# Gathers of a message-passing kernel that also wait for VectorE, another order of its last steps, and a smaller general path

## The chip, the cores and the metric

The kernel runs on one core of a Trainium2 chip. Its engines are TensorE (PE in the profile, with weight loads as PEld), VectorE (DVE), ScalarE (ACT), GpSimd (POOL) and SyncE (SP, which here issues DMAs). The metric is the device time of one execution in microseconds (us); lower is better. Before the change three runs took 722.56, 722.97 and 724.59 us, so the median is 722.97.

## The reference

One graph layer with a residual and a layer norm; 12,500 nodes of 128 features, 400,000 edges sorted by their destination:

```python
rbf = exp(-(distances[:, None] - centers) ** 2 / (2.0 * width * width))      # 50 centres
cut = 0.5 * (cos(pi * distances / CUTOFF) + 1.0) * (distances <= CUTOFF)
W = (silu(rbf @ fw1 + fb1) @ fw2 + fb2) * cut[:, None]
messages = (h[src] @ pw + pb) * W
agg = segment_sum(messages, dst, num_segments=num_atoms)
return h + (silu(agg @ mw1 + mb1) @ mw2 + mb2)
...
x = layernorm(x + that)
```

71,145 of the 400,000 edges lie within the cutoff of 10 in these inputs; all others contribute nothing.

## The kernel before

**Packing.** DVE reads the edge lists in seven chunks, keeps the edges within the cutoff and writes them, packed, to DRAM by seven indirect scatters of POOL. They come back as index columns (`srci`), as cosine factors (`cut`) and as places in a window of nodes (`dl`, `base_i`). Beside it PE multiplies all of x by `pw` and stores the result as `proj` in DRAM.

**Quads.** The packed edges are worked through in 139 quads (NL) of 512 edges, numbered q = 0 to 138. `fetch(q)` gathers the rows of x (the first 12 quads) or of `proj` by four indirect DMAs of 128 rows each, issued by POOL (L1069); for a dozen quads the first of the four is fetched row by row by SP or ACT instead. So POOL has 544 gathers in all, and 7 scatters. 13 buffers (`quad_sb`) take turns, and a gather waits until its buffer has been read. For each quad there are:
- `basis` and `first` (per pair of quads): ACT makes the 50 radial functions, PE the first layer (L1133); `silu` is ACT's (L1139, result `s`).
- `second(q)`: PE's second layer into one PSUM bank, a bias matmul (L1148) and four matmuls (L1151).
- `message(q)`: DVE multiplies that bank by the gathered rows (L1166; L1163 for rows fetched singly).
- `place(q)`: DVE writes four one-hot matrices of 128 edges by a window of nodes, already times `cut` (L1178).
- `sum_up(q)`: PE multiplies message by one-hot into `sums` (L1198).
- `add(q)`: DVE adds `sums` to `aggT`, the table of all nodes in SBUF, at positions loaded into registers from `base_i`. `bases_of` loads many values at once (L1207).

**Nodes.** Where all edges of a block of node tiles are summed, `node_first` (PE L1242/L1243, then ACT's silu into `zs`, L1245), `node_second` (PE L341/L344), `node_stats` (DVE L1280, L1284), `deviations` (L1291 to L1300), `scales` (L1310/L1311), `normal`, which normalizes (ACT, L1331), and `store` (L187) follow. The last blocks are those that start at node tiles 80, 84, 88, 90, 92, 94 and 96.

**Order.** The engines run their instructions in the order in which the program writes them. A planner with estimated times writes quads 0 to 131. The last seven, 132 to 138, are written out by hand, as a list of calls (L1610 to L1718): step q sums quad q, computes `second(q+2)` and places quad q+1, with node work in between. Each step begins with `house(q)`, which fetches and loads ahead.

**Banks.** `second`, `node_first` and `node_second` take their PSUM bank from a list of four free ones (`bank_167` to `bank_170`), in the order in which the program takes and frees them. The bank of `node_first` goes back to the list when its `zs` is written down, and whoever takes it next waits on the chip until ACT has read it:

```python
nc.scalar.activation(in_turn(s[:, :n], n), by_tile(pz[:, :n], n), AF.Silu)
free.append(pz)
```

**General path.** Behind the hand-written steps stands `with tc.If(some > 0, label="over")` (L1792): code for inputs with more or differently spread near edges than the packed lists hold. With these inputs it isn't entered; each engine compares and jumps over it. It is unrolled.

Of the kernel before, what the change touches and what calls it, by code (L numbers as in the profile page):

```python
# [9 lines left out]

F32 = mybir.dt.float32
BF16 = mybir.dt.bfloat16
# [3 lines left out]
OP = mybir.AluOpType  # L16
# [71 lines left out]
def kernel(  # L88
# [90 lines left out]

        return v.rearrange("f (t p) -> f t p", p=P) if n % P == 0 else v  # L180

    def node_dma(t0, sb, dr, store, n=None, eng=nc.sync):

        for a, m, k in alike(rows(t0, n)):
            d = dr[(t0 + a) * P:(t0 + a) * P + m * k].rearrange("(p t) f -> p t f", p=k)
            s = sb[:k, a:a + m]
            eng.dma_start(d, s) if store else eng.dma_start(s, d)  # L187

# [239 lines left out]
    def place_of(q):  # L428
        n, later = LATER
        return q % len(quad_sb) if q < n else later[(q - n) % len(later)]  # L430

    def before_it(q):

        return max((m for m in range(q) if place_of(m) == place_of(q)), default=-1)

    def room(q):

# [625 lines left out]
    def fetch(q, idx=None, table=None, js=range(QT)):  # L1063
        got = quad_sb[place_of(q) if q >= 0 else 0]
        for j in js:
            if q in SINGLY and j == 0:
                continue
            i = srci[:, 2 * q + j // 2, j % 2:j % 2 + 1] if idx is None else idx[:, j:j + 1]
            nc.gpsimd.indirect_dma_start(  # L1069
                out=got[:, j, :], out_offset=None, in_=proj if table is None else table,  # L1070
                in_offset=bass.IndirectOffsetOnAxis(ap=i, axis=0))
        got_of[q] = got

    def quads(o):
# [3 lines left out]
    def radial(o, lengths):  # L1078

        n = math.prod(lengths.shape) // QE  # L1080
        v = lengths.rearrange("(o h) e -> o h e", o=1)
        if o < 0:
            d = quad_sb[1].rearrange("p j f -> p (j f)")
            nc.sync.dma_start(d, v.to_broadcast([64, 2, QE]))
# [149 lines left out]

    zs_of, py_of, done = {}, {}, [0]

    def node_first(t0):

        n = sum(rows(t0))
        assert done[0] == NL or t0 * P + n <= done_to(2 * done[0])  # L1240
        pz = bank()
        nc.tensor.matmul(pz[:, :n], bias_b["mb1"][:, 0, :], ones_b[:, :n], start=True, stop=False)  # L1242
        nc.tensor.matmul(pz[:, :n], mw1_sb, aggT[:, t0 * P:t0 * P + n], start=False, stop=True)  # L1243
        s = work.tile([P, QE], F32, name="zs", tag="hp", bufs=3)
        nc.scalar.activation(in_turn(s[:, :n], n), by_tile(pz[:, :n], n), AF.Silu)  # L1245
        free.append(pz)
        zs_of[t0] = s
# [55 lines left out]
    def deviations(group, st):  # L1303
        return roots(*variances(group, st))
# [33 lines left out]
        nc.vector.memset(st, 0.0)  # L1338
        return st

    def finish(every):

        for t0 in every:
            load_x(t0)
            st = statistics()
            node_first(t0)
            node_second(t0)
            node_stats(t0, st)
            scales(*deviations([t0], st))
            normalize(*ready.pop(0))  # L1350
        store()


    begin, at_q = {}, NODES
# [279 lines left out]
    node_first(88)  # L1634
# [46 lines left out]
    sum_up(p, msg)  # L1681
    node_second(92)
    sum_up(q, message(q, (0, 1)), (0,))
    add(p)
# [32 lines left out]
    normalize(*ready.pop(0), on=(0, 1), eng=nc.scalar)  # L1717
    store()  # L1718

    def more(q):  # L1720
# [12 lines left out]
        base_of(q)  # L1733
        add(q)

    def everything():
        nc.vector.memset(aggT, 0.0)
        def again(e0, seen):

            def column(ap, dt, name):  # L1740
                t = work.tile([P, QT], dt, name=name, bufs=1)
                nc.sync.dma_start(t, ap[ds(e0, QE)].rearrange("(j p) -> p j", p=P))
                return t

            idx = column(src, I32, "idx")
            loc_i = column(dst, I32, "loc_i")
            lengths = column(edge_weight, F32, "lengths")
            loc = work.tile([P, QT], F32, name="loc", bufs=1)
            nc.vector.tensor_copy(loc, loc_i)
            wgt = work.tile([P, QT], F32, name="wgt", bufs=1)  # L1750
            near = work.tile([P, QT], F32, name="near", bufs=1)
            nc.vector.tensor_scalar(near, lengths, CUTOFF, 0.5, op0=OP.is_le, op1=OP.mult)
            if seen:
                nc.vector.memset(near[:, :seen], 0.0)
            fold(wgt, lengths, work.tile([P, QT], F32, name="fold_f", bufs=1),
                 work.tile([P, QT], I32, name="fold_i", bufs=1))
            cosine(wgt)
            nc.vector.scalar_tensor_tensor(wgt, wgt, 1.0, near, op0=OP.add, op1=OP.mult)
            fetch(-2, idx)
            radial(-1, edge_weight[ds(e0, QE)].rearrange("(o e) -> o e", o=1))  # L1760
            basis(-1)
            first(-1)
            silu(-1)
            second(-2)
            u = own(0, "msg", 0)
            for j in range(QT):
                nc.vector.tensor_scalar(u[:, j, :], pu_of[-2][:, j * H:(j + 1) * H],
                                        wgt[:, j:j + 1], None, op0=OP.mult)
            free.append(pu_of.pop(-2))
            msg = own(1, "msg", 0)  # L1770
            nc.vector.tensor_mul(msg, u, got_of.pop(-2))
            for n0 in range(0, N, WS):
                n = min(WS, N - n0)
                at = work.tile([P, QT], F32, name="at")
                nc.vector.tensor_scalar(at, loc, float(-n0), None, op0=OP.add)
                pa = bank()
                for j in range(QT):
                    hot = quad_sb[2 + j % 2].rearrange("p j f -> p (j f)")[:, :WS]
                    nc.vector.tensor_scalar(hot[:, :n], iota_n[:, :n], at[:, j:j + 1],
                                            None, op0=OP.is_equal)  # L1780
                    nc.tensor.matmul(pa[:, :n], msg[:, j, :], hot[:, :n],
                                     start=(j == 0), stop=(j == QT - 1))
                nc.vector.tensor_add(aggT[:, n0:n0 + n], aggT[:, n0:n0 + n], pa[:, :n])
# [8 lines left out]
    with tc.If(some > 0, label="over"):  # L1792
        total = nc.values_load(bad_i[0:1, 0:1], min_val=0, max_val=2 * E)
        extra = nc.values_load(bad_i[0:1, 1:2], min_val=0, max_val=E)
        with tc.If(extra > 0):
            for q in range(NL, NQ):
                more(q)
            finish(blocks)
        with tc.If(total > 0):
            everything()  # L1800


# [24 lines left out]
```

## Time and profile before

| | before |
|---|---|
| median of three runs | 722.97 us (722.56 to 724.59) |
| the profiled execution | 722.04 us, of which 720.2 us are the span of the trace |
| busy, share of the span | PE 82%, PEld 65%, DVE 78%, ACT 56%, POOL 73% |
| POOL instructions | 565 |
| TensorE clock granted, mean | 0.91 |
| moved by DMA | 91.44 MB |

The page of the profile shows one execution. It gives the busy time of each engine, then groups of instructions by line with their count, their busy time, the mean time of one in ns, and the idle time of the engine just ahead of them with what ended it; "issue" means that nothing in the profile released the instruction. The windows view gives an engine's busy time and count in stretches of the span, followed by the mean TensorE clock, the share of time for which the DMA engines were busy and GB/s. The timeline lists single instructions or short runs of alike ones: start, duration, engine, line, operation, out<-in, count, and in brackets the idle time ahead with its releaser. The view of one line gives the least, median and greatest duration in ns and the first and last start. An engine's name with a q (SPq, DVEq) is its sequencer: branches, waits, register loads, DMA issues.

### The profile page before, as it was taken

The numbers are of one execution on the slowest core, as the hardware profiler recorded it, in microseconds if no ns is written. First come the engines' busy times: TensorE is split into PE (matmuls) and PEld (weight loads), VectorE is DVE, ScalarE is ACT, GpSimd is POOL, SyncE is SP. The second block draws the span as 40 slices with busy tenths as digits, with TensorE's granted clock in tenths as the row PEclk, the third lists the DMA queues.
The fourth block names the chain that finished last, engine by engine and source line by source line (L and its number), as shares of the span: only waits on it lengthen the run. The fifth ranks groups of instructions, "written<-read, shape, count | busy, mean of one in ns | idle before, by whom it ended". The sixth has DMA issues, their size and how long they took to land.

```text
span 720.2 us, 14506 instructions
## 1 busy us (share of the span) xinstructions
PE 589.1 (82%) x3526; PEld 466.7 (65%) x3526; DVE 560.7 (78%) x1741; ACT 401.9 (56%) x569; POOL 528.8 (73%) x565
## 2 busy tenths in 40 slices
PE   6787668778988798798878997799998877978783
PEld 5676457666766576576666775577785665756663
DVE  8789999759998889989979994866855545655764
ACT  7356825144744667654644566466765742674554
POOL 6767777777777777777777777777777777777770
PEclk9799996799999899989997999699999897999997
DMA  8898453243434223443334344444443434344242
GB/s 284 264 287 264 114 159 103 59 139 83 115 103 129 86 84 86 129 131 84 86 111 118 101 114 121 131 127 126 143 121 92 142 100 113 99 142 126 56 130 77
DMA packets 54008, 91.44 MB, mean 127 GB/s; under 512 B 14273, under 2 KB 21537, under 8 KB 53915
## 3 DMA queue, kind: packets, MB, share of 16 engines
q0 software_dynamic: 17712, 36.51, 20.4%
q1 hardware_dynamic: 24916, 35.61, 15.0%
q10 hardware_dynamic: 11286, 18.31, 8.1%
q8 instruction: 29, 0.48, 0.3%
q14 instruction: 65, 0.52, 0.2%
HBM read 74.59 MB, written 15.79 MB: 125 GB/s over the span
## 4 chain that ended last, share of the span: by engine, by line
DVE 23%; PE 17%; POOL 17%; DMA 14%; issue 13%; ACT 3%; DVEq 2%; ACTq 1%; SPq 0%; POOLq 0%
POOL quad L1069 13%; DMA quad<-proj,srci 10%; DVE hot L1178 5%; PE ph L1133 4%; PE bank L1151 4%; POOL x L1069 4%; DVE msg L1166 3%; PE sums L1198 3%; PE bank L344 2%; DMA x<-proj,srci 2%; DVE aggT L1232 1%; DVEq L1207 1%; DMA pair<-packed 1%; DMA packed<-line,at_i 1%; DVE bank L516 1%
## 5 line engine op out<-in xcount | busy, mean ns | idle before, releaser
L1069 POOL DMA_INDIRECT quad<-proj,srci x402 | 382.3, 951 | 122.7 <-issue 98.3
L1151 PEld LDWEIGHTS bank<-fw_sb,s 128*128 128x128 f32 x1112 | 157.8, 205 | 56.7 <-issue 46.4
L1151 PE MATMUL bank<-fw_sb,s 128*128 128x128 f32 x1112 | 157.8, 288 | 0.0
L1133 PE MATMUL ph<-rbf,w_sb 102*128 102x512 f32 x278 | 143.8, 642 | 11.0 <-ACT s L1139 6.6
L1198 PEld LDWEIGHTS sums<-hot,msg 128*128 128x128 f32 x816 | 111.2, 203 | 48.8 <-issue 26.3
L1139 ACT ACTIVATE s<-ph 128x1024 f32<-128x1024 f32 x70 | 71.3, 1018 | 125.8 <-PE ph L1133 125.5
L1178 DVE TENSOR_SCALAR hot<-iota_n,dl,cut 128x80 f32<-128x80 f32 (+4 forms) x408 | 109.2, 341 | 23.3 <-PE sums L1198 20.0
L1198 PE MATMUL sums<-hot,msg 128*128 128x80 f32 (+4 forms) x816 | 113.4, 285 | 10.7 <-DVE msg L1166 10.4
L1069 POOL DMA_INDIRECT x<-proj,srci x94 | 90.0, 958 | 28.9 <-issue 25.9
L1148 PE MATMUL bank<-fb_b,ones_b 96*128 96x512 bf16 x139 | 56.0, 403 | 39.3 <-DVE msg L1166 22.9
L1133 PEld LDWEIGHTS ph<-rbf,w_sb 102*128 102x128 f32 x278 | 51.4, 206 | 51.0 <-issue 37.8
L1166 DVE TENSOR_TENSOR msg<-bank,quad 128x512 f32<-128x512 f32 (+1 forms) x78 | 52.4, 672 | 39.9 <-DMA quad<-proj,srci 33.6
L1232 DVE TENSOR_TENSOR aggT<-aggT,sums 128x80 f32 (+4 forms) x209 | 53.8, 258 | 29.5 <-PE sums L1198 10.4
L1117 ACT ACTIVATE rbf<-d_sb,rbf_bias,rbf_scale 102x512 f32<-102x512 f32 x70 | 56.2, 803 | 7.8 <-issue 7.8
L1069 POOL DMA_INDIRECT quad<-in_x_dram,srci x48 | 46.7, 973 | 18.0 <-issue 12.8
L344 PEld LDWEIGHTS bank<-pw_sb,xT 128*128 128x128 f32 (+1 forms) x292 | 44.1, 218 | 15.2 <-ACT xT L976 8.3
L1198 PE MATMUL sums<-quad,quad 128*128 128x128 f32 (+3 forms) x296 | 43.2, 291 | 10.8 <-DVE quad L1166 10.8
L1139 ACT ACT_TABLE_LOAD x34 | 43.6, 1283 | 15.1 <-issue 14.8
L1121 ACT ACT_TABLE_LOAD x35 | 44.9, 1283 | 11.3 <-issue 9.5
L1121 ACT ACTIVATE rbf<-rbf 102x512 f32<-102x512 f32 x70 | 44.1, 630 | 7.9 <-issue 5.5
L1198 PEld LDWEIGHTS sums<-quad,quad 128*128 128x128 f32 x296 | 39.8, 207 | 12.5 <-DVE quad L1166 12.2
L344 PE MATMUL bank<-pw_sb,xT 128*128 128x128 f32 (+1 forms) x292 | 45.0, 303 | 0.6 <-ACT xT L976 0.4
(281 smaller groups left out, 797.7 us busy)
## 6 DMA issues: line engine op xcount, KB each, us to landing
d_sb<-near_d ACTq DMA_DIRECT2D x67, 256.0 KB
row_sb<-proj SPq DMA_DIRECT2D x1024, 0.5 KB
x<-in_x_dram SPq DMA_DIRECT2D x46, 256.0 KB
row_sb<-proj ACTq DMA_DIRECT2D x512, 0.5 KB
quad<-proj,srci POOLq DMA_INDIRECT x402
proj<-hp SPq DMA_DIRECT2D x24, 256.0 KB
out_dram<-x SPq DMA_DIRECT2D x22, 256.0 KB
x<-proj,srci POOLq DMA_INDIRECT x94
```

The lines of the kernel that those rows point to most:

```text
L344: nc.tensor.matmul(to[:m, k, :], lT[:, k * P:k * P + m], w, start=False, stop=(k == a + c - 1))
L1069: nc.gpsimd.indirect_dma_start(out=got[:, j, :], out_offset=None, in_=proj if table is None else table, in_offset=bass.IndirectOffsetOnAxi ...
L1117: a = nc.scalar.activation(rbf[:u], d[:u], AF.Square, bias=rbf_bias[:u], scale=rbf_scale[:u])
L1121: nc.scalar.activation(rbf[:u], rbf[:u], AF.Exp, scale=-1.0 / (2.0 * width * width))
L1133: nc.tensor.matmul(ph[:, h, :], w1_sb[:2 * KR, h, :], rbf[:2 * KR], start=True, stop=True)
L1139: nc.scalar.activation(s[:, :n], ph[:, :n], AF.Silu)
L1148: nc.tensor.matmul(pu, ones_b[:, :P], bias_b["fb2"].rearrange("k j f -> k (j f)"), start=True, stop=False)
L1151: nc.tensor.matmul(pu[:, j * H:(j + 1) * H], s[:, j * P:(j + 1) * P], fw2_sb, start=False, stop=(j == QT - 1))
L1166: nc.vector.tensor_mul(msg[:, a:b, :], pu_of[q].rearrange("p (j f) -> p j f", j=QT)[:, a:b, :], got_of[q][:, a:b, :])
L1178: nc.vector.tensor_scalar(hot[:, j, :wide(q)], iota_n[:, :wide(q)], dl[:, at[0], at[1]], cut[:, at[0], at[1]], op0=OP.is_equal, op1=OP.mult)
L1198: nc.tensor.matmul(pa[:, k * W:k * W + wide(q)], msg[:, j, :], hot[:, j, :wide(q)], start=(j % n == 0), stop=(j % n == n - 1))
L1232: nc.vector.tensor_add(to, to, pa[:, k * W:k * W + wide(q)])
```

## The change

It has three parts.

**1. Waits.** A callback logs every DVE instruction of six kinds as the program writes it. Each gather with q from 0 to 138 gets a dependency on the DVE instruction that stands `behind(q)` places before the last one logged. The table `BACK` sets the number of places: 66 from quad 0 on, 38 from 16, 46 from 26, 38 from 39, 26 from 52, 19 from 63, 46 from 88, 14 from 102 and 8 from 111.

```diff
+BACK = ((0, 66), (16, 38), (26, 46), (39, 38), (52, 26), (63, 19), (88, 46), (102, 14),
+        (111, 8))
+UPTO = NL
+VECTORS = ("TensorScalarPtr", "TensorTensor", "CopyPredicated", "TensorReduce", "TensorCopy",
+           "BNStats")
...
+        if i.engine == mybir.EngineType.DVE and str(i.opcode) in VECTORS:
+            vectors.append(i.name)
...
-            nc.gpsimd.indirect_dma_start(
+            g = nc.gpsimd.indirect_dma_start(
...
+            if 0 <= q < UPTO and len(vectors) > behind(q):
+                tc.add_manual_dep(
+                    g.ins, vectors[-1 - behind(q)],
+                    mybir.DependencyInfo(mybir.DependencyClass.Sync, mybir.DependencyReason.DATA))
```

No engine's instruction order changes by this, up to quad 131 nothing but the waits differs. A gather that already waited for a later DVE instruction keeps its wait. Of 551 gathers and scatters 150 have other waits than before; their number in all goes from 741 to 752.

**2. The last steps.** Calls of the hand-written list stand in another order; `bases_of` loads the 14 positions of all seven quads in step 132 instead of six there and eight in step 135.

```diff
     q = NL - 7
...
-    node_second(84)
     second(q + 2)
-    bases_of([q, q + 1, q + 2])
+    bases_of(list(range(q, NL)))
     place(q + 1)
     scales(*deep.pop(0))
     add(q)
-    normal(1)
     first(octs(q))
     silu(octs(q))
+    node_second(84)
+    normal(1)
...
     sum_up(q, message(q))
-    normal(1)
     second(q + 2)
     first(octs(q))
     silu(octs(q))
+    normal(1)
     place(q + 1)
...
     sum_up(q, message(q))
+    second(q + 2)
     node_second(88)
-    second(q + 2)
     place(q + 1)
...
     sum_up(q, message(q))
+    second(q + 2)
     node_second(90)
-    second(q + 2)
-    bases_of([q, q + 1, q + 2, q + 3])
     place(q + 1)
...
     add(q)
+    node_first(92)
     scales(*dev)
-    node_first(92)
     normal(1)
-
-    tc.mark_branch_hint_location("over")
+    place(q + 2)
+
     p, q = NL - 2, NL - 1
     house(p)
-    msg = message(p)
-    place(q)
-    sum_up(p, msg)
+    sum_up(p, message(p))
```

ACT in steps 132 to 134, before (`x41` and `x42` are the normalizations of `normal`, `s` the results of `silu`, `zs_10850` that of `node_first(88)`):

```order
L1245 ACTIVATE zs_10755<-bank1_168 128x512
L1331 ACTIVATE x41_87<-x41_87,by_10795,rs_10794 128x128 x4
L1139 ACTIVATE s_10808<-ph_10805 128x1024
L1331 ACTIVATE x42_88<-x42_88,by_10795,rs_10794 128x128 x4
L1139 ACTIVATE s_10840<-ph_10838 128x512
L1245 ACTIVATE zs_10850<-bank3_170 128x256
```

and now:

```order
L1270 ACTIVATE zs_10755<-bank1_168 128x512
L1162 ACTIVATE s_10814<-ph_10811 128x1024
L1356 ACTIVATE x41_87<-x41_87,by_10806,rs_10805 128x128 x4
L1162 ACTIVATE s_10851<-ph_10849 128x512
L1356 ACTIVATE x42_88<-x42_88,by_10806,rs_10805 128x128 x4
L1270 ACTIVATE zs_10866<-bank3_170 128x256
```

Each set of four normalizations has moved behind the silu that it preceded, so that the second set stands directly ahead of the last zs.

PE from the end of step 133 through step 134, before (`mb2`, `mw2`: `node_second(88)`; `fb2`, `fw2`: `second(136)`):

```order
L1242 MATMUL bank3_170<-ones_b_130,mb1_b_134 128x256
L1243 MATMUL bank3_170<-aggT_99,mw1_sb_119 128x256
L1198 MATMUL sums_10865<-quad6_79,quad4_77 128x128 x4
L341 MATMUL bank3_170<-mb2_b_135,ones_b_130 128x256
L344 MATMUL bank3_170<-mw2_sb_120,zs_10850 128x128 x2
L1148 MATMUL bank1_168<-fb2_b_133,ones_b_130 128x512
L1151 MATMUL bank1_168<-fw2_sb_118,s_10808 128x128 x4
```

and now:

```order
L1267 MATMUL bank3_170<-ones_b_130,mb1_b_134 128x256
L1268 MATMUL bank3_170<-aggT_99,mw1_sb_119 128x256
L1221 MATMUL sums_10881<-quad6_79,quad4_77 128x128 x4
L1171 MATMUL bank3_170<-fb2_b_133,ones_b_130 128x512
L1174 MATMUL bank3_170<-fw2_sb_118,s_10814 128x128 x4
L347 MATMUL bank0_167<-mb2_b_135,ones_b_130 128x256
L350 MATMUL bank0_167<-mw2_sb_120,zs_10866 128x128 x2
```

The two have changed places, and with them the banks: `second(136)` now writes `bank3_170`, which `node_first(88)` wrote and its zs reads.

DVE in steps 136 and 137, before (`msg1_680` is the message of quad 137, `quad6_79` the one-hot of quad 138):

```order
L1310 RECIPROCAL rs_10995<-dev_10968 128x12
L1311 SCALAR_TENSOR_TENSOR by_10996<-both_m_10961,rs_10995 128x12
L1166 TENSOR_TENSOR msg1_680<-bank3_170,quad2_75 128x512
L1178 TENSOR_SCALAR quad6_79<-iota_n_145,dl_158,cut_157 128x128 x4
L1166 TENSOR_TENSOR quad4_77<-bank2_169,quad3_76 128x128
```

and now:

```order
L1335 RECIPROCAL rs_10998<-dev_10967 128x12
L1336 SCALAR_TENSOR_TENSOR by_10999<-both_m_10960,rs_10998 128x12
L1201 TENSOR_SCALAR quad6_79<-iota_n_145,dl_158,cut_157 128x128 x4
L1189 TENSOR_TENSOR msg1_680<-bank1_168,quad2_75 128x512
L1189 TENSOR_TENSOR quad4_77<-bank2_169,quad3_76 128x128
```

The one-hot of the last quad stands ahead of the message of the one before it.

**3. The general path.** `finish` (the node phases once more), the sums over windows and the walk over all edges become hardware loops, with DMAs by POOL; the label "over" and its hint are gone.

```diff
+    def finish_all():
+
+        with tc.For_i(0, N // (4 * P), 1) as block:
+            finish(0, block * (4 * P))
...
-            for n0 in range(0, N, WS):
...
+            with tc.For_i(0, N // WS, 1) as w:
...
-        with tc.For_i(0, E // QE, 1) as g:
-            again(g * QE, 0)
-        if E % QE:
-            again(E - QE, QT - E % QE // P)
-        finish(blocks)
-
-    with tc.If(some > 0, label="over"):
+        with tc.For_i(0, steps, 1) as g:
+            again(smin(g * QE, E - QE))
+
+    with tc.If(some > 0):
```

In the built program the instructions between each engine's branch and the place where it lands change from 262 to 111 on SP, from 541 to 123 on ACT, from 1083 to 174 on DVE, from 749 to 146 on PE and from 74 to 152 on POOL. POOL has four register moves more at its start. The hint left no instruction on the path that is taken.

More of the change, by code (lines that the diff above doesn't have):

```diff
@@ L9 @@
 from concourse._compat import with_exitstack
+from concourse.expressions import smin
 F32 = mybir.dt.float32
@@ L434, in before_it, with logged, behind @@
         return max((m for m in range(q) if place_of(m) == place_of(q)), default=-1)
+    vectors = []
+    def logged(i):
+        if i.engine == mybir.EngineType.DVE and str(i.opcode) in VECTORS:
+            vectors.append(i.name)
+    nc.push_inst_callback(logged)
+    def behind(q):
+        return next(n for at, n in reversed(BACK) if q >= at)
     def room(q):
@@ L1083, in radial @@
             d = quad_sb[1].rearrange("p j f -> p (j f)")
-            nc.sync.dma_start(d, v.to_broadcast([64, 2, QE]))
+            nc.gpsimd.dma_start(d, v.to_broadcast([64, 2, QE]))
         else:
@@ L1235, with node_first @@
     zs_of, py_of, done = {}, {}, [0]
-    def node_first(t0):
+    def node_first(t0, sums=None):
         n = sum(rows(t0))
-        assert done[0] == NL or t0 * P + n <= done_to(2 * done[0])
+        if sums is None:
+            assert done[0] == NL or t0 * P + n <= done_to(2 * done[0])
+            sums = aggT[:, t0 * P:t0 * P + n]
         pz = bank()
         nc.tensor.matmul(pz[:, :n], bias_b["mb1"][:, 0, :], ones_b[:, :n], start=True, stop=False)
-        nc.tensor.matmul(pz[:, :n], mw1_sb, aggT[:, t0 * P:t0 * P + n], start=False, stop=True)
+        nc.tensor.matmul(pz[:, :n], mw1_sb, sums, start=False, stop=True)
         s = work.tile([P, QE], F32, name="zs", tag="hp", bufs=3)
@@ L1339, in statistics, with finish @@
         return st
[L1341 to L1351, printed above, removed]
+    def finish(t0, at):
+        n = sum(rows(t0))
+        y = x_sb[t0] = x4_sb[0]
+        node_dma(t0, y, x, False, eng=nc.gpsimd, at=at)
+        sums = quad_sb[OTHERS[0]].rearrange("p j f -> p (j f)")[:, :n]
+        nc.vector.tensor_copy(sums, aggT[:, ds(at, n)])
+        st = statistics()
+        node_first(t0, sums)
+        node_second(t0)
+        node_stats(t0, st)
+        scales(*deviations([t0], st))
+        _, rs, by = ready.pop(0)
+        for k in range(len(rows(t0))):
+            scaled(t0, y, rs, by, k, False)
+        node_dma(t0, x_sb.pop(t0), out, True, eng=nc.gpsimd, at=at)
+    def finish_all():
+        with tc.For_i(0, N // (4 * P), 1) as block:
+            finish(0, block * (4 * P))
+        if N % (4 * P):
+            t0 = N // (4 * P) * 4
+            finish(t0, t0 * P)
     begin, at_q = {}, NODES
@@ L1718 @@
     store()
+    nc.remove_inst_callback(logged)
     def more(q):
@@ L1737, in everything, with again @@
         nc.vector.memset(aggT, 0.0)
-        def again(e0, seen):
+        steps, seen = -(-E // QE), -E % QE // P
+        left = work.tile([P, 1], F32, name="left", bufs=1)
+        nc.vector.memset(left, float(steps - 1))
+        def again(e0):
             def column(ap, dt, name):
                 t = work.tile([P, QT], dt, name=name, bufs=1)
-                nc.sync.dma_start(t, ap[ds(e0, QE)].rearrange("(j p) -> p j", p=P))
+                nc.gpsimd.dma_start(t, ap[ds(e0, QE)].rearrange("(j p) -> p j", p=P))
                 return t
@@ L1753, in again @@
             if seen:
-                nc.vector.memset(near[:, :seen], 0.0)
+                last = work.tile([P, 1], F32, name="last", bufs=1)
+                nc.vector.tensor_scalar(last, left, 1.0, None, op0=OP.min)
+                nc.vector.tensor_scalar(near[:, :seen], near[:, :seen], last, None, op0=OP.mult)
+                nc.vector.tensor_scalar(left, left, -1.0, None, op0=OP.add)
             fold(wgt, lengths, work.tile([P, QT], F32, name="fold_f", bufs=1),
@@ L1771, in again @@
             nc.vector.tensor_mul(msg, u, got_of.pop(-2))
-            for n0 in range(0, N, WS):
-                n = min(WS, N - n0)
-                at = work.tile([P, QT], F32, name="at")
-                nc.vector.tensor_scalar(at, loc, float(-n0), None, op0=OP.add)
+            assert N % WS == 0
+            with tc.For_i(0, N // WS, 1) as w:
                 pa = bank()
@@ L1778, in again @@
                     hot = quad_sb[2 + j % 2].rearrange("p j f -> p (j f)")[:, :WS]
[L1779 to L1783, printed above, removed]
-                free.append(pa)
-        with tc.For_i(0, E // QE, 1) as g:
-            again(g * QE, 0)
-        if E % QE:
-            again(E - QE, QT - E % QE // P)
-        finish(blocks)
-    with tc.If(some > 0, label="over"):
+                    nc.vector.tensor_scalar(hot, iota_n, loc[:, j:j + 1], None, op0=OP.is_equal)
+                    nc.tensor.matmul(pa[:, :WS], msg[:, j, :], hot, start=(j == 0),
+                                     stop=(j == QT - 1))
+                to = aggT[:, ds(w * WS, WS)]
+                nc.vector.tensor_add(to, to, pa[:, :WS])
+                nc.vector.tensor_scalar(loc, loc, -float(WS), None, op0=OP.add)
+                free.append(pa)
+        with tc.For_i(0, steps, 1) as g:
+            again(smin(g * QE, E - QE))
+    with tc.If(some > 0):
         total = nc.values_load(bad_i[0:1, 0:1], min_val=0, max_val=2 * E)
```

6 lines of the change are left out of this document (3 added, 3 removed).

## The prediction

> **What bounds the kernel now.** I read the page's costliest groups first, then the windows view for the gather line alone.
>
> ```profile
> L1069 POOL DMA_INDIRECT quad<-proj,srci x402 | 382.3, 951 | 122.7 <-issue 98.3
> 100.00:200.00 100.00, 74.58 (x80) 0.85 0.35 96
> ...
> 600.00:700.00 100.00, 75.61 (x81) 0.91 0.39 108
> L1069 POOL DMA_INDIRECT quad<-proj,srci x402: 940/945/1254, 73.1 to 702.3; - x134
> ```
>
> In the first row the idle time ahead of a gather is put down to "issue": nothing released it, it is POOL's own gap. A gather takes 0.945 us (the median of the last row), and a window of 100 us holds 80 or 81 of them at its two ends, so one comes every 1.25 us with 0.30 us of gap. POOL therefore sets the pace from the first gathers to 702.3 us, whatever DVE, PE and ACT do in between, and TensorE's clock (0.85 and 0.91 in the same rows) matters little there. Only what follows the last gathers, some 20 us, is bound by other things.
>
> The program's own time here is 722.04 us for a span of 720.2 us. The median of the runs shown is 722.97, 0.93 us above the profiled execution. I sum on 722.04 and add 0.93 at the end.
>
> **Part 1: the waits on VectorE.** POOL issues the same gathers in the same order. The built programs differ in the waits of 150 gathers: each of these now waits for a later DVE instruction than its buffer asks for. What is behind a gather on POOL is nothing but more gathers, so a wait that ends late shifts all that follow. I laid each newly named DVE instruction beside its gather; the narrowest place is this one:
>
> ```profile
> 672.87 0.68 DVE L1280 SCALAR_TENSOR_TENSOR x<-x,bank 128x512 f32<-128x512 f32 x1
> 679.67 0.95 POOL L1069 DMA_INDIRECT quad<-proj,srci  x1 [0.30 <-DVE by L1311]
> ```
>
> The DVE instruction ends at 673.55, 6.1 us before the gather starts. Elsewhere the margin is larger. The gather above keeps the usual gap of 0.30 us, as gathers without a DVE event ahead of them do, so a wait that is already met costs nothing. Term: **0**. Its bounds: 0 while DVE stays within 6.1 us of its place beside POOL, and beyond that one microsecond for each further one (rival C). A gain is excluded: the gap of 0.30 us stays, and a wait makes no gather shorter.
>
> **Part 2: the order of the last steps.** A step bears the number of its quad, 132 to 138. In steps 132 and 133:
>
> ```profile
> 680.77 0.60 ACT L1245 ACTIVATE zs<-bank 128x512 f32<-128x512 f32 x1
> 681.42 0.38 PE L341 MATMUL bank<-mb_b,ones_b 96*128 96x512 bf16 x1 [2.28 <-ACT zs L1245]
> 682.39 1.10 DVE L1178 TENSOR_SCALAR quad<-iota_n,dl,cut 128x128 f32<-128x128 f32 x4
> 686.99 1.05 PE L1198 MATMUL sums<-hot,msg 128*128 128x128 f32 x8
> 688.11 1.63 ACT L1331 ACTIVATE x<-x,by,rs 128x128 f32<-128x128 f32 x4
> 690.05 0.60 ACT L1139 ACTIVATE s<-ph 128x512 f32<-128x512 f32 x1 [0.31 <-PE ph L1133]
> 690.60 0.39 ACT L1245 ACTIVATE zs<-bank 128x256 f32<-128x256 f32 x1
> ```
>
> PE waits 2.28 us for the ACT step that makes zs of tiles 84 to 87. Putting second(134) ahead of node_second(84) looks like a way round that wait, but the bank that second(134) then takes is the one which that same zs reads and frees. PE still starts at about 681.4: nothing is won. sum_up(133) still comes behind the same sum of PE work. On ACT, the silu of 512 columns at 690.05 now stands ahead of the four normalizations of 688.11. It cannot start sooner, since it waits for PE, so those 1.63 us now lie between it and the zs of tiles 88 and 89: that zs moves from 690.60 to 690.65 + 1.63 = 692.3, and its end from 691.0 to about 692.7.
>
> ```profile
> 691.68 0.27 PE L341 MATMUL bank<-mb_b,ones_b 96*128 96x256 bf16 x1
> 691.79 0.61 PE L344 MATMUL bank<-mw_sb,zs 128*128 128x128 f32 x4
> 692.24 0.38 PE L1148 MATMUL bank<-fb_b,ones_b 96*128 96x512 bf16 x1
> 692.46 1.05 PE L1151 MATMUL bank<-fw_sb,s 128*128 128x128 f32 x8
> 692.49 0.42 DVE L1280 SCALAR_TENSOR_TENSOR x<-x,bank 128x256 f32<-128x256 f32 x1
> 693.53 0.69 DVE L1166 TENSOR_TENSOR quad<-bank,quad 128x512 f32<-128x512 f32 x1
> ```
>
> In step 134 second(136), 692.24 to 693.51, goes ahead of node_second(88), 691.68 to 692.40. second(136) now takes the bank that the late zs frees, so it starts at about 692.8 and ends at 694.1; node_second(88) ends near 694.8. DVE's statistics of tile 88 go from 692.49 to about 694.8, and message(135), queued behind them on DVE, from 693.53 to about 695.7: **+2.2** there.
>
> ```profile
> 695.79 1.21 DVE L1178 TENSOR_SCALAR hot<-iota_n,dl,cut 128x128 f32<-128x128 f32 x4 [1.57 <-issue]
> 696.83 0.60 DVE L1232 TENSOR_TENSOR aggT<-aggT,sums 128x128 f32 x2
> 697.34 0.41 DVE L1280 SCALAR_TENSOR_TENSOR x<-x,bank 128x256 f32<-128x256 f32 x1
> 698.92 0.69 DVE L1166 TENSOR_TENSOR msg<-bank,quad 128x512 f32<-128x512 f32 x1
> L1207 DVEq TENSOR_LOAD <-base_i x63: 339/508/2133, 107.3 to 693.6; - x63
> L1041 ACTq TENSOR_LOAD <-at_row x32: 1197/1304/1608, 145.2 to 627.0; - x32
> ```
>
> The hole of 1.57 us ahead of 695.79 is DVE's load of eight values (2133 ns, the longest of the load's row). It goes, since one load of 14 values in step 132 serves all. That load isn't in the trace. The same line's median is 0.51 us for fewer values, ACT's load of 16 takes 1.30 and the eight took 2.13, so it lies between 0.5 and some 3.7 us (14/8 of 2.13). I take 1.3, by the row nearest in values. It stands ahead of place(133), which ended at 683.49 and which PE needs only at sum_up(133), at 686.99: 3.5 us of cover. A load of six already stands there, so at most 3.7 less 0.5 come on, which the cover holds. Without the hole place(136) follows message(135) at 696.4 and add(135) comes at about 697.6, so +2.2 shrinks to +0.8. But second(137) now stands ahead of node_second(90) too: message(135) ends at 696.4, sum_up(135) takes PE to about 697.4, second(137) to 698.6 and node_second(90) to 699.2. The statistics of tile 90 wait for that (697.34 before), with the four short instructions after them, and message(136) goes from 698.92 to about 700.6: **+1.7**. The gain of the load is spent on node_second.
>
> ```profile
> 701.82 0.69 DVE L1166 TENSOR_TENSOR msg<-bank,quad 128x512 f32<-128x512 f32 x1
> 702.43 1.13 DVE L1178 TENSOR_SCALAR quad<-iota_n,dl,cut 128x128 f32<-128x128 f32 x4
> 703.31 1.05 PE L1198 MATMUL sums<-hot,msg 128*128 128x128 f32 x8
> 706.23 0.48 DVE L1166 TENSOR_TENSOR quad<-bank,quad 128x128 f32<-128x128 f32 x2
> ```
>
> In steps 136 and 137 place(138), 1.13 us at 702.43, moves ahead of message(137), 701.82. Both are needed, but before, PE summed quad 137 while DVE placed 138. Now message(137) starts at about 701.82 + 1.7 + 1.1 less some 0.3 of idle time that closes = 704.3, and sum_up(137) at about 705.1: **+1.8**. place(138) is then out of the way, so it doesn't grow further. The last gather's rows arrived before 706.23 (its message had DVE as its limit), so it hides nothing. Term: **+1.8**, which reaches the end undiminished, as nothing idles behind it. Bounds: +1.2 to +3.5. The upper end is for where the low clock falls:
>
> ```profile
> 683.47 1.92 PE L1151 MATMUL bank<-fw_sb,s 128*128 128x128 f32 x8
> ```
>
> The same eight matmuls as those at 692.46 (1.05 us) took 1.92 us here, so PE runs at about half for some 3 us. If that stretch meets second(136) and node_second(88), which are newly on the path, it adds some 0.9 + 0.7 us.
>
> **Part 3: the general path made small.** It isn't entered; each engine jumps over it. SP's jump skips 111 instructions instead of 262, ACT's 123 instead of 541, DVE's 174 instead of 1083, POOL's 152 instead of 74.
>
> ```profile
> L1792 SPq COMPARE_BRANCH  x1: 50/50/50, 713.5 to 713.5; - x1
> L1792 SPq EVENT_SEMAPHORE  x9: 17/17/17, 717.5 to 718.1; - x9
> L1792 ACTq COMPARE_BRANCH  x1: 54/54/54, 713.7 to 713.7; - x1
> L1792 ACTq EVENT_SEMAPHORE  x2: 17/17/17, 716.9 to 717.0; - x2
> L1792 POOLq COMPARE_BRANCH  x1: 53/53/53, 696.1 to 696.1; - x1
> L1792 POOLq EVENT_SEMAPHORE  x5: 17/43/43, 696.3 to 704.9; - x5
> ...
> GB/s 0 35 0 0 0 0 0 0 35 77 190 249 319 196 284 249 40 22 40 79 15 24 22 0 0 0 0 35 0 0 35 0 0 0 0 0 0 0 0 0
> ```
>
> SP runs its next instruction 4.0 us after its branch, ACT 3.2 us, POOL only 0.2 us: a jump of 74 is free, one of 262 is not. SP's first wait after the jump is at 717.5, its ninth at 718.1, and the span ends 2.1 us later, at 720.2. The last row is bytes moved in forty slices from 711 to 720.3 us, 0.2325 us each: output flows in bulk up to slice 16 (714.7) and in drops up to slice 23 (716.35). So if SP's jump becomes free, SP waits for the stores instead and the end comes 717.5 - 716.35 = 1.2 us sooner, or, if the drops too stem from the instruction transfers that share the engines, up to 717.5 - 714.95 = 2.5 us. 111 is nearer to 74 than to 262, so I take the jump as free. ACT's jump of 123 should be free with it; if it alone is not, its 717.0 still binds and 0.6 us is the gain. Term: **-1.7**, between 1.2 and 2.5; for a jump that still misses, 0.
>
> [...]
>
> The loops of the general path add four register moves to POOL's start, before a barrier that all engines wait for.
>
> ```profile
> 0.74 0.20 POOL masks.py:197 MEMSET ident<- 128x128 f32 x1 [0.29 <-POOLq L1815]
> ```
>
> POOL's four memsets start 0.26 to 0.35 us in and its first work behind the barrier at 0.74. A register move should be no dearer than the 0.07 us that lies between other short sequencer instructions (nine waits of SP take 0.6 us): 4 x 0.07 = **+0.3**, with 0 as the other end.
>
> **Sum.** 722.04 + 0 + 1.8 - 1.7 + 0.3 = 722.4; with 0.93, **723.4** against the median of 722.97. Bounds of the terms: 1.2 - 2.5 + 0 = -1.3, and 3.5 - 1.2 + 0.3 = +2.6, so 721.7 to 725.6.
>
> **Rivals.**
> [...]
> B. The new order helps. For it: PE idles 2.28 us at 681.42 and DVE 1.57 us at 695.79. If tiles 88 and 90 don't hold up messages (the zs of tile 88 on time, or DVE's statistics not waited for), what stays is the load's 1.57 us less place(138)'s 1.1 in front: -0.5 - 1.7 + 0.3 = -1.9: **721.1**, and 719.2 where the 1.57 come through whole and the jump brings 2.5 (-1.6 - 2.5 + 0.3).
> C. Slower by the waits: in the last 28 quads a gather waits for a DVE instruction only eight places back. If DVE runs more than 6.1 us later beside POOL than in this trace, POOL stops, and nothing behind makes it up. Each gather queue that moves back also delays the messages on which DVE itself waits, so it can repeat: at 9 us of lag 2.9 us come on, **726.3**. Against it: the margin was 6.1 us at its least in this execution, and DVE idles at many places in the tail above.
> D. No effect at all: the waits met, the tail hidden, the jump unchanged: **723.0**.
>
> **Chances.** Forecast 0.48, A 0.20, B 0.18, C 0.09, D 0.05. A measurement of this kernel can tell about 0.3%, 2.2 us, from no change: below 720.8 is faster, above 725.1 slower. The forecast's bounds put 0.04 of its 0.48 above 725.1 and the rest within; of A half is above; of B two thirds are below, C is above but for 0.01, D within. Faster 0.12, slower 0.04 + 0.10 + 0.08 = 0.22, within 0.66. The range for 8 in 10 runs from 720.3, which takes in part of B, to 726.2, which takes in A but for its low clock, and leaves C out.
>
> **What would show it.** Right: gathers still 80 to a window of 100 us, with gaps of 0.30 us and the last at about 702.5; zs of tile 88 near 692.3, message(135) near 695.7, message(136) near 700.6, sum_up(137) near 705.1; SP's first instruction after its branch waiting on a store rather than 4 us. Wrong: gathers with gaps of a microsecond that end on DVE (C); 4 us still there after SP's branch (A); message(136) at 699 or before (B).

## The result and the profile after

The changed kernel takes 720.83 us, the median of 22 runs (717.74 to 722.80), and before 721.58 us, also of 22 (719.19 to 724.59): a ratio of 0.999, 95% interval 0.9978 to 1.0003. That is no change that can be told, which was the forecast; its 723.4 us was 2.6 us too high. The median of before was 722.97 with the three runs known at that time, so 1.4 us of the miss is their scatter, and 1.2 us lies in the terms. The profiled execution took 720.8 us for a span of 719.2. Ratios, here and below, leave out executions over 1.5% longer than the fastest of their kernel, so a ratio can differ from that of the two medians.

The gathers first: the line of the gather on the page of the changed kernel, the windows for that line, and the line's own view (L1088 is L1069 of before).

```profile
L1088 POOL DMA_INDIRECT quad<-proj,srci x402 | 381.8, 950 | 122.6 <-issue 99.1
100.00:200.00 100.00, 74.82 (x79) 0.86 0.34 95
600.00:700.00 100.00, 75.62 (x81) 0.95 0.38 107
L1088 POOL DMA_INDIRECT quad<-proj,srci x402: 940/945/1191, 72.2 to 700.9; - x134
```

Nothing moved: 0.945 us for one, 79 to 81 in 100 us, all but 23.5 us of the idle time without a releaser. POOL is still the bound, and the new waits are met before their gathers come up: in the view of POOL's waits only the first gather waits longer than 0.3 us.

Next the last steps, in the timeline of the changed kernel. Its zs of tiles 84 to 87 starts at 679.35, 1.4 us sooner than before (680.77), so 1.4 is taken off each row of before in the comparison.

```profile
679.35 0.60 ACT L1270 ACTIVATE zs<-bank 128x512 f32<-128x512 f32 x1
679.99 0.38 PE L1171 MATMUL bank<-fb_b,ones_b 96*128 96x512 bf16 x1 [2.17 <-ACT zs L1270]
690.72 0.36 ACT L1270 ACTIVATE zs<-bank 128x256 f32<-128x256 f32 x1
691.14 0.38 PE L1171 MATMUL bank<-fb_b,ones_b 96*128 96x512 bf16 x1 [0.66 <-ACT zs L1270]
692.24 0.27 PE L347 MATMUL bank<-mb_b,ones_b 96*128 96x256 bf16 x1
694.43 0.69 DVE L1189 TENSOR_TENSOR quad<-bank,quad 128x512 f32<-128x512 f32 x1 [0.49 <-issue]
698.04 0.42 DVE L1305 SCALAR_TENSOR_TENSOR x<-x,bank 128x256 f32<-128x256 f32 x1 [1.05 <-PE bank L350]
699.64 0.69 DVE L1189 TENSOR_TENSOR msg<-bank,quad 128x512 f32<-128x512 f32 x1
701.67 1.91 PE L1174 MATMUL bank<-fw_sb,s 128*128 128x128 f32 x8
703.48 0.68 DVE L1189 TENSOR_TENSOR msg<-bank,quad 128x512 f32<-128x512 f32 x1
705.67 1.05 PE L1221 MATMUL sums<-hot,msg 128*128 128x128 f32 x8
708.59 0.48 DVE L1189 TENSOR_TENSOR quad<-bank,quad 128x128 f32<-128x128 f32 x2
```

PE waits for the zs as before (2.17 us), now with second(134) in front. The zs of tile 88 is 1.5 us later than before beside the first, second(136) waits for it (0.66 us), message(135) at 694.43 is 2.3 us late, message(136) at 699.64 is 2.1 late and waits behind the statistics of tile 90 (698.04), which wait for PE. At 701.67 the low clock falls in (0.50 to 0.57 granted from 701.5 to 705.0, 1.00 on both sides): eight matmuls take 1.91 us. sum_up(137) at 705.67, 703.31 before, is then 3.8 us late, and the last part of message(138) too.

Last the jumps over the general path (L1832 is L1792 of before).

```profile
L1832 SPq COMPARE_BRANCH  x1: 50/50/50, 716.0 to 716.0; - x1
L1832 SPq EVENT_SEMAPHORE  x1: 17/17/17, 716.2 to 716.2; - x1
L1832 ACTq COMPARE_BRANCH  x1: 50/50/50, 716.0 to 716.0; - x1
L1832 ACTq EVENT_SEMAPHORE  x2: 17/17/17, 716.5 to 716.6; - x2
L1832 DVEq COMPARE_BRANCH  x1: 76/76/76, 714.7 to 714.7; - x1
L1832 DVEq EVENT_SEMAPHORE  x2: 21/21/21, 717.3 to 717.4; - x2
```

SP goes on 0.2 us after its branch (4.0 before) and has one wait there instead of nine; ACT goes on after 0.5 us (3.2 before). DVE, whose jump shrank most, still takes 2.6 us and is now the last. SP branches 3.2 us before the span's end, 6.7 us before it in the old trace. So 3.8 us were lost in the last steps and 3.5 gained behind them, and the 1.4 us by which these steps began sooner make the span 1.0 us shorter.

Two of the three chips on which the experiments ran take 1074 us for the kernel before, the third 720; each kernel is compared with before on its own chip.

### The profile page after: what moved, and what is told of

Same layout as the page of the kernel before. It is cut to its first block, busy times and chain, and to the rows that moved or that the text cites. A ratio compares the mean times of both kernels' runs of the same rounds, so it can differ in the third digit from the quotient of the medians.

```text
span 719.2 us, 14505 instructions
## 1 busy us (share of the span) xinstructions
PE 585.5 (81%) x3526; PEld 459.7 (64%) x3526; DVE 561.4 (78%) x1741; ACT 401.6 (56%) x569; POOL 529.7 (74%) x565
## 5 line engine op out<-in xcount | busy, mean ns | idle before, releaser
L1088 POOL DMA_INDIRECT quad<-proj,srci x402 | 381.8, 950 | 122.6 <-issue 99.1
L1156 PE MATMUL ph<-rbf,w_sb 102*128 102x512 f32 x278 | 147.6, 657 | 11.9 <-ACT s L1162 7.2
L1088 POOL DMA_INDIRECT x<-proj,srci x94 | 90.4, 962 | 28.6 <-issue 21.9
L1171 PE MATMUL bank<-fb_b,ones_b 96*128 96x512 bf16 x139 | 55.7, 401 | 42.4 <-DVE msg L1189 23.5
L1088 POOL DMA_INDIRECT quad<-in_x_dram,srci x48 | 47.7, 993 | 15.9 <-issue 12.2
L350 PEld LDWEIGHTS bank<-pw_sb,xT 128*128 128x128 f32 (+1 forms) x292 | 40.9, 203 | 11.0 <-issue 4.9
L1356 ACT ACTIVATE x<-x,by,rs 128x128 f32<-128x128 f32 x94 | 38.3, 482 | 8.5 <-issue 3.2
```

The source lines that it names most:

```text
L350: nc.tensor.matmul(to[:m, k, :], lT[:, k * P:k * P + m], w, start=False, stop=(k == a + c - 1))
L1088: g = nc.gpsimd.indirect_dma_start(out=got[:, j, :], out_offset=None, in_=proj if table is None else table, in_offset=bass.IndirectOffsetO ...
L1156: nc.tensor.matmul(ph[:, h, :], w1_sb[:2 * KR, h, :], rbf[:2 * KR], start=True, stop=True)
L1171: nc.tensor.matmul(pu, ones_b[:, :P], bias_b["fb2"].rearrange("k j f -> k (j f)"), start=True, stop=False)
```

## The experiments

**The new order alone** (first chip, then second): the diff of the last steps, with its one load of 14 positions, without the other two parts.

> The kernel before with the new order of the last steps alone. Theory (the order costs, the small path pays): +1.8 to +3.7 us against before; message(136) some 2 us and sum_up(137) 1.8 to 3.7 us later beside the last gather than before, SP still 4 us in its jump. Rival (each part does nothing that can be told): within 0.7 us. Rival (the order helps): -1 us or less.

Measured: 1075.93 us against 1074.0, ratio 1.0026 (0.9994 to 1.0058).

> The new order of the last steps alone, once more, on a chip on which POOL is the bound (on the first one the kernel before took 1074 us). Theory: +1.8 to +3.7 us against before. Rival (nothing that can be told): within 0.7 us. Rival (the order helps): -1 us or less.

Measured: 1074.96 us against 1073.58, ratio 0.9998 (0.9967 to 1.0029). The second chip was no better suited than the first, and +1 to +2 us in 1074 can't be told from nothing. But on these chips the last gather starts some 16 us before the zs of tile 84, and the trace of the last steps stands undisturbed, here on the second chip:

```profile
1035.57 0.60 ACT L1245 ACTIVATE zs<-bank 128x512 f32<-128x512 f32 x1
1045.25 0.36 ACT L1245 ACTIVATE zs<-bank 128x256 f32<-128x256 f32 x1
1045.67 0.38 PE L1148 MATMUL bank<-fb_b,ones_b 96*128 96x512 bf16 x1 [0.66 <-ACT zs L1245]
1048.85 0.69 DVE L1166 TENSOR_TENSOR quad<-bank,quad 128x512 f32<-128x512 f32 x1 [0.38 <-issue]
1054.07 0.69 DVE L1166 TENSOR_TENSOR msg<-bank,quad 128x512 f32<-128x512 f32 x1
1058.64 1.16 PE L1198 MATMUL sums<-hot,msg 128*128 128x128 f32 x8
```

From the zs of tile 84 it is 9.7 us to that of tile 88, 13.3 to message(135), 18.5 to message(136) and 23.1 to sum_up(137) in the last row, with the same 0.66 us of PE's wait as in the changed kernel.

**The small general path alone** (first and second chip): `finish`, `again` and `everything` as loops, nothing else.

> The kernel before with the small general path alone. Theory: from the last store's issue to the end 3.2 us instead of 6.7, less 0.25 us at the start: -3.2 us against before, and SP's jump 0.2 us instead of 4.0. Rival (nothing that can be told): within 0.7 us.

Measured: 1068.5 us against 1074.0, ratio 0.9975 (0.9939 to 1.0011).

> The small general path alone, once more, for the same reason. Theory: -3.2 us against before. Rival (nothing that can be told): within 0.7 us.

Measured: 1075.19 us against 1073.58, ratio 0.999 (0.9951 to 1.0029). Again the time can't tell; the trace can. The jump in the second run, and the same steps as above in the first, in the order of before:

```profile
L1810 SPq COMPARE_BRANCH  x1: 50/50/50, 1066.5 to 1066.5; - x1
L1810 SPq EVENT_SEMAPHORE  x1: 17/17/17, 1066.7 to 1066.7; - x1
```

```profile
1030.00 0.60 ACT L1248 ACTIVATE zs<-bank 128x512 f32<-128x512 f32 x1
1038.19 0.38 ACT L1248 ACTIVATE zs<-bank 128x256 f32<-128x256 f32 x1
1041.12 0.69 DVE L1167 TENSOR_TENSOR quad<-bank,quad 128x512 f32<-128x512 f32 x1
1046.43 0.69 DVE L1167 TENSOR_TENSOR msg<-bank,quad 128x512 f32<-128x512 f32 x1
```

SP goes on after 0.2 us. In the old order it is 8.2 us from zs to zs, 11.1 to message(135) and 16.4 to message(136): the new order with its one load costs 1.5, 2.2 and 2.1 us at these places, with no low clock in either stretch as far as the matmuls show it: eight of `second` take 1.05 us each time.

**The small path and the one load of 14 positions**, old order, no waits (first and second chip):

```diff
-    bases_of([q, q + 1, q + 2])
+    bases_of(list(range(q, NL)))
...
-    bases_of([q, q + 1, q + 2, q + 3])
```

> The small general path and the one load of 14 positions, in the order of before, without the waits. Theory: the small path's -3.2 us and most of the 1.57 us for which DVE idled behind the load of eight, so -4 to -4.8 us against before and faster than the changed kernel by 3 us or more. Rival (the hole was no bound, something else is late next): -3.2 us as with the small path alone. Rival (the path does nothing): within 0.7 us.

Measured: 1071.91 us against 1074.0, ratio 0.9953 (0.9908 to 0.9998).

> The small general path and the one load of 14 positions in the order of before, without the waits, once more. Theory: -4 to -4.8 us against before. Rival (something else is late next): -3.2 us as with the small path alone. Rival: within 0.7 us.

Measured: 1066.57 us against 1073.58, ratio 0.9934 (0.9899 to 0.997). By time the first run is hardly to be told from before, its median being 0.2% lower, and the second gained 7 us where 4.8 were expected; so again the trace decides. message(136) of the second run:

```profile
1031.72 0.60 ACT L1248 ACTIVATE zs<-bank 128x512 f32<-128x512 f32 x1
1042.85 0.69 DVE L1167 TENSOR_TENSOR quad<-bank,quad 128x512 f32<-128x512 f32 x1
1046.97 0.69 DVE L1167 TENSOR_TENSOR msg<-bank,quad 128x512 f32<-128x512 f32 x1
```

message(135) comes as in the old order (11.1 us after the zs), message(136) after 15.3 instead of 16.4: the load brings 1.2 us of its 1.57. Against this kernel, which has the load too, the new order costs 3.2 us at message(136) (18.5 against 15.3).

**The waits alone, and with all counts halved** (first and second chip): the first diff of the change, and then with the table

```diff
+BACK = ((0, 33), (16, 19), (26, 23), (39, 19), (52, 13), (63, 9), (88, 23), (102, 7),
+        (111, 4))
```

> The kernel before with the gathers' waits alone. Theory (all met): 0 within 0.7 us, gathers 1.25 us apart. Rival (the waits order the early gathers better: the gathers of the changed kernel ended 1.4 us sooner than those of before): -1.4 us. Rival (they stall POOL): gaps over 0.4 us that end on DVE, +1 us or more.

Measured: 1070.85 us against 1074.0, ratio 0.9871 (0.9826 to 0.9916). The medians differ by 0.3% alone, so no gain is shown by this run.

> The kernel before with the waits alone, every count of the table halved (66 to 33, 38 to 19, down to 8 to 4). Beside the trace of before 14 gathers would then start before the VectorE instruction that they wait for ends, the worst by 3.8 us (at 73 us), and none after 200 us. Theory (a wait costs what it ends too late, once for all that follow, and nothing where it is met): +3 to +5 us against before, with gaps on POOL that end on DVE before 200 us and none later. Rival (a lagging VectorE is delayed again by the late gathers, and so on): +8 us or more. Rival (later waits spare some other contention): 0 or faster.

Measured: 1060.25 us against 1073.58, ratio 0.9871 (0.9832 to 0.9909). The theory was for a chip on which POOL is the bound, and fails here: on these chips it isn't (57 to 65 POOL instructions in each 100 us from 600 to 1000 with the order alone on this chip, against 80 or 81 gathers in 100 us of the trace of before, on a chip of 720). What came is the last rival, 0 or faster: each of these six runs (up to 1064.86 us) took less than any of before (from 1065.28). The gathers end later, the last at 1034.4 us where it is 1019.1 with the order alone. See the last section.

**The waits at their nearest** (`BACK = ((0, 0),)`, third chip, 720 us before):

> The kernel before with waits on the very last VectorE instruction logged (all counts 0). Where before runs in 721 us: POOL stalls, worst shortfall beside the trace of before 15.7 us, so +15 us or more. On a chip where before runs in 1074 us and halving the counts brought -13 us: theory (what pays is that POOL doesn't run ahead) a gain of 13 us or more again; rival (a gather that starts too late is waited for): the gain is lost, 0 or slower.

Measured: 768.22 us against 720.15, ratio 1.064 (1.0607 to 1.0674): +48 us. POOL's waits (line waited for: us in total, times, longest), then two windows of all its work:

```profile
POOL quad L1086 <- issue: 113.0, 356, 3.0
POOL quad L1086 <- DMA near_d<-length: 9.1, 1, 9.1
POOL quad L1086 <- DVE quad L1187: 7.4, 4, 3.5
POOL quad L1086 <- DVE sums L601: 6.8, 1, 6.8
```

```profile
100.00:200.00 100.00, 66.28 (x71) 0.83 0.31 90
...
600.00:700.00 100.00, 75.60 (x81) 0.90 0.43 118
```

In the second hundred only 71 gathers come instead of 80, with single waits of 3.0 to 4.5 us between them (the 9.1 us lie elsewhere); from 600 on the pace is the old one. The last gather starts at 748.7 instead of 702.3 us. The sum is three times the worst single shortfall of 15.7 us. The reading that fits is that of rival C: a late gather delays VectorE, whose next instruction holds the next gather, and so on; no run takes this chain apart. This is the price that the table's larger counts keep away from.

**The changed kernel and the changed kernel in the old order**, together on the third chip. The second puts the hand-written steps back and keeps the one load, the waits and the small path:

```diff
     sum_up(q, message(q))
-    second(q + 2)
     node_second(88)
+    second(q + 2)
...
-    place(q + 2)
...
-    sum_up(p, message(p))
+    msg = message(p)
+    place(q)
+    sum_up(p, msg)
```

and so at the other places.

> The changed kernel itself, timed beside before on a chip of the experiments. If that chip runs before in some 1074 us like the first two: the sum of the parts as measured there, waits -3 to -13, path -3, order +1.6, so -4 to -14 us. Rival (only the tail counts, the waits' gain was scatter): -1 to -2 us. If before runs in some 721 us: -0.7 us.

Measured: 719.98 us against 720.15, ratio 0.9995 (0.9977 to 1.0012).

> The changed kernel with the order of before in its last steps; the one load of 14 positions, the waits and the small path stay. Theory (the order costs 1.6 us and hides the load's 1.2 or more): 2.8 to 4.5 us faster than the changed kernel, on any chip; from the zs of tile 84 to the last store's issue about 30 us instead of 34.5 to 36.6. Rival (the order of the changed kernel is what makes the load pay): equal to the changed kernel or slower.

Measured: 715.42 us against 720.15, ratio 0.9926 (0.9902 to 0.9951), 4.6 us faster than the changed kernel on the same chip. Its last steps:

```profile
679.10 0.60 ACT L1270 ACTIVATE zs<-bank 128x512 f32<-128x512 f32 x1
687.30 0.39 ACT L1270 ACTIVATE zs<-bank 128x256 f32<-128x256 f32 x1
690.22 0.69 DVE L1189 TENSOR_TENSOR quad<-bank,quad 128x512 f32<-128x512 f32 x1
694.36 0.69 DVE L1189 TENSOR_TENSOR msg<-bank,quad 128x512 f32<-128x512 f32 x1
698.35 0.69 DVE L1189 TENSOR_TENSOR msg<-bank,quad 128x512 f32<-128x512 f32 x1 [1.09 <-DMA quad<-proj,srci]
700.55 0.94 POOL L1088 DMA_INDIRECT quad<-proj,srci  x1 [0.30 <-issue]
```

zs of tile 88 after 8.2 us, message(135) after 11.1, message(136) after 15.3: the distances of the second chip to 0.1 us. message(137) now waits 1.09 us for its gathered rows. The last steps have caught up with POOL here, so a shorter message(136) would gain nothing at this place. From the zs of tile 84 to SP's branch it is 30.7 us here and 34.7 in the changed kernel on the same chip. The parts as measured, -3.5 for the small path (of the profiled executions), +0.2 at the start and -1.2 for the load, add up, as an estimate, to -4.5 us against before; the times say -4.7. This version beats both kernels.

**Without the gathers from quad 26 on** (third chip). The messages of these quads use rows that the buffers still hold; all other work stays.

```diff
             if q in SINGLY and j == 0:
                 continue
+            if q >= 26:
+                continue
```

> The kernel before without the gathers from quad 26 on (the messages of these quads then use rows left in the buffers); all arithmetic stays. On a chip where before runs in 721 us POOL no longer is the bound: PE's 589 us of work and its waits, 640 to 700 us. On a chip at 1074 us, theory (POOL's gathers disturb the other engines there): 850 us or less, with DVE's and ACT's waits for late PE results gone after quad 26. Rival (PE pauses there by itself): 1000 us or more, the pauses as before.

Measured: 674.92 us against 720.15, ratio 0.9335 (0.9291 to 0.9379). It was meant for the chips at 1074 us and tells nothing on those. It shows how much POOL is the bound here: without most gathers the same arithmetic takes 45 us less.

## Why the prediction was right

**The waits: right.** Term 0, and the gathers kept 1.25 us each. This rests on the traces: the waits alone ran only on chips of 1074 us. That the last gather came 1.4 us sooner in the profiled execution after (700.9 against 702.3) is not owed to the waits as far as was seen: it was 701.6 and 700.6 in two others with the same waits. There is one trace of before on such a chip, so this isn't settled. That unmet waits cost time, as in rival C, the nearest waits show, more dearly than I had it (46 us of late gathers from 15.7 of shortfall, not one for one).

**The order: right in its steps, low in its size.** All links held: no gain from the first exchange, the silu ahead of the normalizations, the bank, the message behind the statistics. The places:

| | forecast | profile after, against before | order alone, against the old order |
|---|---|---|---|
| zs of tile 88 | +1.7 | +1.5 | +1.5 |
| message(135) | +2.2 | +2.3 | +2.2 |
| message(136) | +1.7 | +2.1 | +2.1 |
| sum_up(137) | +1.8 | +3.8 | some +2.2 (estimate) |

The old order in the last column is that of the small path alone, with its two loads. In the last row the changed kernel lies beyond the upper bound of the forecast, +3.5: the low clock fell into the newly critical work, but at 701.7, on second(138) and the matmuls of node_x(96), not on second(136) as I had drawn it. From message(137) to sum_up(137) it takes 2.19 us there and 0.74 with the order alone, so some 1.5 of the 3.8 are the low clock's. The estimate for the rest: 23.1 us after the zs of tile 84 with the order alone, against 19.7 in the old order with one load and 1.2 more without it. The load of 14 positions took 1.35 us in the changed kernel (1346 ns, the longest of its row), as estimated. What I had not seen is how much it would have brought with the old order: 1.2 us, which the new order hides.

**The small path: right in kind, mis-sized.** The term was -1.7 (1.2 to 2.5). From SP's branch to the span's end it went from 6.7 to 3.2 us, -3.5 in the profiled execution and beyond the upper bound; on the second chip it went from 6.5 (order alone) to 3.3 (path alone). The drops from which the 2.5 was worked out were in part transfers of instructions: of 50 packets from 714.8 to 716.6 in the trace of before two are of q14, of kind instruction (0.02 of 0.05 MB), the others of q1 and q10. I had SP wait for the stores, and it does. But I left all that followed its first wait before, 717.5 to 720.2 or 2.7 us, behind the stores. The first DRAIN stands behind the waits with which SP closes the program (before, then the changed kernel); the other rows are what these waits wait for, in the changed kernel, in this order, and in the second run of the small path alone:

```profile
L1823 SPq DRAIN  x3: 7/7/13, 719.0 to 719.3; - x3
L1863 SPq DRAIN  x3: 7/7/13, 718.2 to 718.6; - x3
SPq L1863 <- DVEq L1832: 0.8, 1, 0.8
SPq L1863 <- DMA out_dram<-x: 0.3, 1, 0.3
SPq L1841 <- DMA out_dram<-x: 1.2, 2, 1.0
```

Before, SP passed its nine waits and the closing ones from 717.5 to 719.0, all behind the jump. Now it passes most of them while the stores are under way, and only 1.0 us is left behind the last store (718.2 to 719.2). DVE's jump, 174 instructions long, takes 2.6 us where 2.9 were taken before. It doesn't set the end: SP waits for it until 717.4, and then for the stores. With the old order this jump takes 1.2 to 1.4 us, SP waits for the stores alone, and from its branch to the end it is no shorter, 3.3 to 3.6 us.

That SP's jump of 111 instructions and ACT's of 123 would be free was an estimate of mine from the rows of before: 0.2 us for POOL's of 74, 4.0 for SP's of 262, 3.2 for ACT's of 541. They now take 0.2 and 0.5 us. DVE's, of 174, takes 2.6 us in the changed kernel and with the same path 1.2 to 1.4 us in the old order, so the length alone doesn't decide. No run shows what does.

**The start: right.** POOL's first work behind the barrier came at 0.97 instead of 0.74 us, +0.23 for a forecast of +0.3.

```profile
0.97 0.20 POOL masks.py:197 MEMSET ident<- 128x128 f32 x1 [0.29 <-POOLq L1855]
```

**The sum.** +1.8 - 1.7 + 0.3 = +0.4 was forecast, and -0.75 measured (medians of 22). The two large terms were both too small, by about 2 us each in the profiled execution, and cancelled; that the sum came so close is in this part luck.

## What to carry to other kernels

Moving work ahead of a wait helps only if it doesn't wait for the same thing: here the banks were handed on in program order, and the moved matmuls took the very bank that the wait was about (2.17 us of it against 2.28). When two edits of opposite sign land together, time each alone: the pair showed nothing, and one of them taken back gave 4.6 us. A dependency added to a saturated queue was free here while it was met (the gathers' gap stayed at 0.30 us); unmet by at most 15.7 us it cost 48.

## What the runs showed of the hardware

The same kernel took 720 us on one chip and 1074 us on two others. With the order alone on the first of those, POOL's longest waits are:

```profile
POOL quad L1069 <- DVE msg L1166: 128.5, 24, 17.6
POOL quad L1069 <- issue: 123.9, 389, 2.9
```

There POOL waits for VectorE's messages too (128.5 us in 24 waits; 1.5 us in 5 in the trace of before, on a chip of 720 us). PE's granted clock was 0.75 to 0.78 there and 0.88 to 0.94 on the third chip, and in the trace of the order alone on the second chip ACT twice started work on PE's results 2 to 8 us after the modelled end of the matmuls, while gathers were under way. Much of what ACT and DVE wait for in that trace the profile ascribes to nothing on this core and calls "remote": 284 us of ACT's idle time (and, on the first chip, 270 of DVE's with the same kernel), of which the longest row is

```profile
ACT s L1139 <- remote: 180.8, 17, 31.4
```

The traces of before and of the changed kernel, on chips of 720 us, have no such row. In the last steps, when all gathers had landed, the distances of the old order with the one load were those of the third chip (15.3 us from the zs of tile 84 to message(136) on both; eight matmuls of `second` take 1.05 us there, so no low clock shows). On the second chip the waits with halved counts went with a faster kernel (ratio 0.9871); with the full counts, on the first chip, no gain is shown. Why ACT starts so late there, what "remote" stands for, and why the kernel with the later gathers was faster, all stay open: the run meant for it was made on the third chip.
